# A message-passing layer with gathered and copied rows: two more tiles copied, and a load moved ahead of two stores

## The chip, the cores and the metric

The kernel runs on one core of one Trainium2 chip. The metric is the device time of one execution in microseconds (us), the median of several runs. A core has five engines that run their own instruction streams and meet at semaphores: TensorE (PE in the profile, its weight loads PEld), VectorE (DVE), ScalarE (ACT), GpSimd (POOL) and SyncE (SP). Here SP issues nearly all plain transfers; GpSimd issues the indirect gathers.

## The reference

There are 12500 nodes with 64 features and 200000 edges, sorted by destination, with 32 features each. Each edge makes a message out of its source's row, its destination's row and its own features; messages are summed at the destinations, each node is updated, and the result is normalized:

```python
msg_in = concat([nodes[row], nodes[col], edge_features])
messages = relu(msg_in @ mW1 + mb1) @ mW2 + mb2
aggregated = segment_sum(messages, col)
upd = relu(concat([nodes, aggregated]) @ uW1 + ub1) @ uW2 + ub2
out = layernorm(x + upd)
```

## The kernel before

**Tiles and groups.** The edges are cut into 1563 tiles of 128, and these into 261 groups of 6 (the last, group 260, has 3). The destinations are sorted, so all edges of a tile fall into a window of 32 nodes. Two tables are made at the start: A = x W1a (for sources) and B = x W1b + b1 (for destinations). For a group, TensorE multiplies one-hot columns of the destinations and the edge features with B's windows and the edge weights (`edge_part`, L367). GpSimd gathers A's rows of the group's 768 sources, one indirect DMA per tile (`gather`, L209), into `xg`. VectorE adds both (L394), ScalarE takes the relu (L395). TensorE then sums the relus into windows of a wide PSUM tile, by a selection matrix (`collect`, counts L424, sums L427).

**Copied tiles.** In some groups, listed in `COPIED`, the last two tiles are not gathered. Their sources' columns of x (a transposed copy lies in SBUF) are copied one by one into a tile `xc`: columns 0 to 63 by ScalarE (`singly`, L338), 64 to 127 by VectorE (`joined`, L345), each after a load of its address into a register (L315). TensorE multiplies `xc` with W1a into the same PSUM tile (L370). In such a group VectorE's add is shorter (L390), and ScalarE has two relus (L391, L392). `COPIED` starts at group 16 and goes on in steps of 3 and 2; before the change it ends at 246, 249, 251, 254. A group's columns are copied over some 2.5 stages, a few stages ahead of it (`portion`).

**Updates.** The nodes are finished in 34 updates (u = 0 to 33). In the end these follow one another every 3 or 4 groups: the sums of update 30 close behind group 250, of 31 behind 254, of 32 behind 257, of 33 behind 260. An update consists of: opening a new PSUM tile (L402, L422) and carrying the overlap of 32 nodes over (`carry`); ScalarE's copies of counts and sums (`close`, L441 and L442); the load of x's columns into `xw` (`columns`, L457, with the first node's number loaded into a register, L455); two dense products (`update`, L464 with `xw` and L465 with the sums); a relu (L470); two products back to rows (`residual`, L478 and L480); `evacuate` (L486), `statistics` (L494, L496), `deviation` (L501), `norm` (L507, L510) and `store` (L518). There are two `xw` tiles, used in turn: update 33 has the one of update 31.

**Order.** The order is written out by hand: a loop over stages s = 0 to 263 issues, on each engine's queue, the relu of group s, the sums of group s - 1, the product of group s + 1, the copies for later groups, and the steps of updates that are due. Gathers run up to some ten groups ahead, as far as buffers are free. SP's queue takes, stage by stage, B's windows (L274), one-hot sources (L225), edge features (L256), columns and stores, in that order of issue. `columns(u)` stands in stage 260 for u = 33, behind the store of update 32; the product of group 254 needs a PSUM slot that the relu (L470) of update 30 frees.

Of the kernel before, what the change touches and what calls it, by code (L numbers as in the profile page):

```python
# [29 lines left out]
NSUB = -(-NT // SUB)  # L30
# [41 lines left out]
YBASE = XBASE + 4 * XCOLS  # L72
FIRST, GAPS = 16, (3, 2)
COPIED = []
while FIRST + sum(GAPS) * (len(COPIED) // len(GAPS)) + sum(GAPS[:len(COPIED) % len(GAPS)]) < NSUB - 6:
    COPIED.append(FIRST + sum(GAPS) * (len(COPIED) // len(GAPS)) + sum(GAPS[:len(COPIED) % len(GAPS)]))
RNDS = -(-len(COPIED) // len(GAPS))
LAST = 4 * (N - 1)
# [3 lines left out]
def updates():  # L82


    def node(s):
        return N * min(1.0, s * SUB * P / E) ** 2
    at = [0]
    for s in range(1, NSUB):
        if s > at[-1] and node(s + 1) - node(at[-1]) > UN - WIN:
            at.append(s)  # L90
    at = [a for a in at if a < NSUB - 32]
    steps = -(-(NSUB - 3 - at[-1]) // 4)
    return at + [at[-1] + -(-(NSUB - 3 - at[-1]) * (i + 1) // steps) for i in range(steps)]


UPD = updates()
# [5 lines left out]
def gnn_kernel(ctx: ExitStack, tc: tile.TileContext, x1T, x, eT, e_rows, src, src_row, dst, dst_row, wlist, wrow, wnext, whalf,  # L102
# [33 lines left out]
    K = len(UPD)  # L136
# [50 lines left out]
    def frees(s):  # L187

        a = (XG + 1) // 2 + s - XG - ROWB
        return min(2 * a + 1, XG - 1) if a < (XG + 1) // 2 else XG + a - (XG + 1) // 2  # L190
# [23 lines left out]
    with tc.tile_pool(name="sup", bufs=2) as sup, tc.tile_pool(name="work", bufs=2) as work, tc.manual_schedule():  # L214
# [33 lines left out]
        def counts(g):  # L248

            SB[g] = S[g].bitcast(BF).rearrange("p k (w h) -> p k w h", h=2)  # L250
# [37 lines left out]
        def columns_list():  # L288

            for r in range(len(GAPS)):  # L290
                v = src_row[:, ((FIRST + sum(GAPS[:r])) * SUB + SUB - 2) * P:]
                nc.sync.dma_start(cols[r * RNDS:(r + 1) * RNDS],
                                  bass.AP(v.tensor, v.offset, [[sum(GAPS) * SUB * P, RNDS], [1, 2 * P]]))
            cv = cols.rearrange("k (b e) -> k b e", b=2)
            for b, base in enumerate((XBASE, YBASE)):
                nc.vector.tensor_scalar(col_a[:, :, b], cv[:, b], 4.0, float(base), op0=ALU.mult, op1=ALU.add)
# [141 lines left out]
        def close(u):  # L438

            ps, pn = sums.pop(u)  # L440
            nc.scalar.copy(xw[u % 2][0:1, :UW], pn)  # L441
            nc.scalar.copy(sums_s[u % 2], ps)  # L442
# [3 lines left out]
        def width(u):  # L446

            return UN if u + 1 < K else UL
# [4 lines left out]
        def columns(u):  # L453

            n0 = nc.values_load(usup[0:1, u:u + 1], engines=[ET.SP], min_val=0, max_val=N - 1,  # L455
                                skip_runtime_bounds_check_because="destinations are node numbers")
            nc.sync.dma_start(xw[u % 2][ONE:, :width(u)], x1T[:, bass.ds(n0, width(u))])  # L457
            us[u] = n0
# [64 lines left out]
        def relative(a, b):  # L523

            wbc = work.tile([P, WCH], I32, name="wbc", tag="tb")
            nc.sync.dma_start(dst_s[:, a:b], dst[:, a:b])
            nc.sync.dma_start(wbc[:, :b - a], wrow[:, a:b].broadcast_to([P, b - a]))
            nc.vector.tensor_tensor(drc[:, a:b], dst_s[:, a:b], wbc[:, :b - a], op=ALU.subtract)

        def halves(a, b):  # L530

            for h in range(2):
                nc.sync.dma_start(wh[64 * h:64 * h + 64, a:b], whalf[h:h + 1, a:b].broadcast_to([64, b - a]))
# [21 lines left out]
        def others(a, b):  # L555

            nc.sync.dma_start(xfull[:D, a:b, HB:], xchunks[:, a:b, HB:])
            nc.sync.dma_start(yfull[D:, a:b, :HB], xchunks[:, a:b, :HB])
            if b == NB // NCH:
                nc.sync.dma_start(xbot[D:, full:], x1T[1:, full:XCOLS])  # L560

        def zeros(i, n):

            w = XCOLS // n
            for t in (xtop[D:], xbot[:D]):
                nc.scalar.activation(t[:, i * w:(i + 1) * w], ident[:D, 0:1].broadcast_to([D, w]), AF.Copy, scale=0.0)
# [100 lines left out]
        def rest(s):  # L667

            if 3 <= s < 9 and s % 2:
                others((s - 3) // 2 * 4, (s - 3) // 2 * 4 + 4)  # L670
            if 3 <= s < 11:
                zeros(s - 3, 8)
            if s == 9:
                columns_list()
            if s == 1:
                relative(8 * SUP, 8 * SUP + WCH)
            elif s == 2:
                relative(8 * SUP + WCH, NT)
                halves(4 * SUP, NTP // 2)
            elif s == BS:  # L680
                nc.sync.dma_start(wa, wrow.rearrange("o (p c) -> (o p) c", c=NSUP))
                nc.sync.dma_start(wb, wnext.rearrange("o (p c) -> (o p) c", c=NSUP))
                nc.scalar.dma_start(w2, mW2)
                nc.scalar.dma_start(u1a, uW1[D:2 * D, :])
                nc.scalar.dma_start(b2c, mb2.rearrange("(f o) -> f o", o=1))
                nc.vector.memset(uz[:D], 0.0)
                nc.vector.memset(ux[:D], 0.0)
                nc.vector.memset(eps, EPS)
                nc.vector.memset(ones, 1.0)
                nc.vector.tensor_copy(ux[D:], ident[D:, D:])  # L690
                nc.scalar.dma_start(uz[D:], uW1[0:D, :])
                nc.scalar.dma_start(ux[ONE:ONE + 1], ub2.rearrange("(o f) -> o f", o=1))
                nc.scalar.dma_start(ub1_s, ub1.rearrange("(f o) -> f o", o=1))
                nc.scalar.dma_start(u2, uW2)
            elif s == BS + 2:
                weights()
                checks()
# [47 lines left out]
        due = {(UPD[u + 1] if u + 1 < K else NSUB) + 1: u for u in range(K)}  # L745
# [10 lines left out]
        for s in range(last + 2):  # L756
            g, j = divmod(s, SUP // SUB)
            while gathered < NSUB and frees(gathered) < s:
                gather(gathered)
                gathered += 1  # L760
            tail = due.get(s - 1) == K - 1

            def earlier(n):

                return next((u for d, u in due.items() if u + 2 < K and s - d == n and (n < 2 or u + 3 < K)), None)
            if tail:
                norm(K - 1)
            if s + 2 < NSUB:
                windows(s + 2)
            if s < NSUB:  # L770
                node_part(s)
                joined(s, 0, 3 if j == 0 and g + 1 < NSUP else 2)
            if s in at_end:
                for stage, u in at_end[s]:
                    stage(u)
            for stage, n in ((evacuate, 2), (statistics, 3), (deviation, 4), (norm, 5)):
                if earlier(n) is not None:
                    stage(earlier(n))
            if 1 <= s <= NSUB:
                collect(s - 1)  # L780
            if s + 1 in due:
                close(due[s + 1])
            if j == 0 and g + 1 < NSUP:
                select(g + 1, s)
                load(g + 1)
                counts(g + 1)
            if j == 1 and g + 2 < NSUP:
                loadd(g + 2)
            if chunks and s >= BS and chunks[0] < NCH + NB * (s + 1 - BS) / (SUP // SUB * (GE - 1) - BS):
                chunk_b(chunks.pop(0), [Bv])  # L790
            if s in due and due[s] + 1 < K:
                carry(due[s] + 1)
            if s in due and due[s] + 2 != K:
                update(due[s])
            if s + 1 < NSUB:
                if s + 1 < XG:
                    transpose(s + 1)
                edge_part(s + 1)
            if earlier(1) is not None:
                residual(earlier(1))  # L800
            if s == UPD[K - 1]:
                update(K - 2)
            if s == UPD[K - 1] + 1:
                residual(K - 2)
            if due.get(s) == K - 1:
                activated(K - 1)
                residual(K - 1)
                statistics(K - 1)
                deviation(K - 1)
            if s + 2 in due:  # L810
                columns(due[s + 2])
            rest(s)
            joined(s, 2 if j == 0 and g + 1 < NSUP else 1, 3 if j == 0 and g + 1 < NSUP else 2)
            singly(s, 0, 1)
            if s in due and due[s] + 2 < K:
                activated(due[s])
            if s == UPD[K - 1]:
                activated(K - 2)
            if tail:
                store(K - 1)  # L820
            if earlier(5) is not None:
                store(earlier(5))
# [170 lines left out]
```

## Time and profile before

| What | us |
|---|---|
| median of 3 runs | 1737.42 |
| lowest and highest run | 1736.82, 1737.85 |
| the profiled execution | 1741.59 |
| its span, first to last instruction | 1739.8 |
| busy TensorE, ScalarE, GpSimd, VectorE | 1448.5, 1468.6, 1301.0, 1056.2 |

The granted clock of TensorE was 0.581 in the mean of the span. How to read the rows below: a row of a timeline has its start and its length in us from the span's start, the engine, the line of the kernel, the operation, what it writes and reads, and in brackets the idle time of the engine before it with what ended it. SPq and POOLq are instructions of a sequencer, which waits or issues. A row of windows has the busy time of each engine in a stretch, and the TensorE clock that was granted in it, where 1.00 is full and 0.50 half. A matmul in 32-bit floats counts as two, so "x12" are a group's 6 tiles.

### The profile page before, as it was taken

What the parts mean: (1) busy time and instruction counts of PE and PEld (TensorE: products, weight loads), DVE (VectorE), ACT (ScalarE), POOL (GpSimd) and SP (SyncE); (2) the same over time, 40 slices, a digit from 0 to 9 for tenths busy, and PEclk for the clock granted to TensorE, in tenths of its full rate; (3) what the DMA queues carried; (4) which work ended last, traced back from release to release, by engine and by line L of the source; (5) the groups of instructions that cost most, each with busy time, mean ns of one, the idle gap of its engine ahead of it and who ended that gap; (6) DMA issues with size and microseconds to landing.
All of it is one profiled execution on the core that took longest, in us unless ns stands there. A gap on an engine that the chain in (4) does not pass through costs nothing.

```text
span 1739.8 us, 46406 instructions
## 1 busy us (share of the span) xinstructions
PE 1448.5 (83%) x9620; PEld 1247.5 (72%) x9620; DVE 1056.2 (61%) x7329; ACT 1468.6 (84%) x6712; POOL 1301.0 (75%) x1380
## 2 busy tenths in 40 slices
PE   3697888888988888887987898888899878899997
PEld 3586777877777767666776776677777767677776
DVE  1526666666665656666665666666667666666643
ACT  0277989999998898998898999998999999899942
POOL 7777777777777777777777777777777777777774
PEclk8585555555555555656555555655556566666656
DMA  8783444433333333333343433443344444443442
GB/s 213 204 175 99 127 112 115 115 97 100 98 101 92 96 97 93 98 102 94 98 107 102 105 108 103 105 107 103 106 106 110 107 109 106 108 112 104 113 112 66
DMA packets 207588, 192.45 MB, mean 111 GB/s; under 512 B 57511, under 2 KB 173409, under 8 KB 207313
## 3 DMA queue, kind: packets, MB, share of 16 engines
q0 software_dynamic: 43872, 87.97, 20.6%
q1 hardware_dynamic: 148896, 92.56, 19.6%
q10 hardware_dynamic: 14546, 8.93, 1.8%
q8 instruction: 91, 1.49, 0.4%
q14 instruction: 183, 1.50, 0.3%
HBM read 171.54 MB, written 17.76 MB: 109 GB/s over the span
## 4 chain that ended last, share of the span: by engine, by line
POOL 41%; issue 24%; DMA 14%; DVE 10%; PE 5%; ACT 2%; DVEq 2%; SPq 1%; ACTq 0%; POOLq 0%
POOL xg L209 41%; DMA xg<-tab_a,src_s 10%; DVE xc L345 3%; DVE h L394 2%; ACT xc L338 2%; PE sums L427 2%; DVEq L315 2%; PE pc L367 1%; DVE l L237 1%; DMA tab_a<-tb 1%; DMA l<-in_dst_row 1%; DMA w1b<-in_mW 1%; DVE h L390 0%; DMA l<-in_eT 0%; DMA xtop<-in_x1T 0%
## 5 line engine op out<-in xcount | busy, mean ns | idle before, releaser
L209 POOL DMA_INDIRECT xg<-tab_a,src_s x1311 | 1242.0, 947 | 399.8 <-issue 372.0
L338 ACT ACTIVATE xc<-xtop,xbot 128x1 f32 x6144 | 1166.2, 280 | 42.2 <-issue 31.7
L345 DVE TENSOR_TENSOR xc<-xtop,xbot 128x1 int32 x6144 | 536.6, 154 | 417.9 <-issue 402.4
L427 PE MATMUL sums<-sel,h 128*128 128x32 f32 x3126 | 638.9, 371 | 20.4 <-ACT h L395 13.9
L427 PEld LDWEIGHTS sums<-sel,h 128*128 128x128 f32 x3126 | 605.3, 294 | 39.1 <-ACT h L395 15.4
L367 PE MATMUL pc<-rhs,l 64*128 64x128 f32 x3126 | 420.0, 415 | 188.7 <-DVE h L394 134.7
L367 PEld LDWEIGHTS pc<-rhs,l 64*128 64x128 f32 x3126 | 349.6, 295 | 253.0 <-DVE h L394 152.3
L395 ACT ACTIVATE h<-h 128x768 f32<-128x768 f32 x156 | 129.6, 831 | 111.6 <-DVE h L394 110.8
L394 DVE TENSOR_TENSOR h<-pc,xg 128x768 f32<-128x768 f32 x156 | 148.0, 949 | 121.8 <-DMA xg<-tab_a,src_s 67.6
L237 DVE TENSOR_TENSOR l<-l,cps 128x768 f32<-128x768 int32 (+1 forms) x134 | 127.8, 953 | 23.4 <-DMA l<-in_dst_row 18.8
L424 PEld LDWEIGHTS <-one 128*1 128x1 bf16 x1563 | 55.9, 83 | 58.7 <-issue 50.7
L424 PE MATMUL cnt<-sel,one 128*1 128x32 bf16 x1563 | 89.2, 187 | 0.4 <-issue 0.3
L390 DVE TENSOR_TENSOR h<-pc,xg 128x512 f32<-128x512 f32 x96 | 66.1, 688 | 25.8 <-DMA xg<-tab_a,src_s 11.5
L243 DVE TENSOR_TENSOR sel<-cps,drc 128x384 f32<-128x384 f32 x131 | 71.6, 547 | 14.9 <-PE sums L427 14.7
L464 PE MATMUL pu<-xw,uz 128*128 128x448 f32 (+1 forms) x68 | 61.8, 1012 | 17.3 <-DVE h L394 13.6
L370 PE MATMUL pc<-w1a,xc 64*128 64x128 f32 x384 | 75.0, 398 | 0.0
L209 POOL DMA_INDIRECT xg<-in_x,src_s x60 | 58.0, 967 | 19.1 <-issue 17.7
L391 ACT ACTIVATE h<-h 128x512 f32<-128x512 f32 x96 | 59.2, 617 | 10.4 <-DVE h L390 9.5
L370 PEld LDWEIGHTS pc<-w1a,xc 64*128 64x128 f32 x384 | 66.7, 311 | 0.0
L583 ACT COPY tb<-pb 128x512 f32<-128x512 f32 (+1 forms) x13 | 7.4, 570 | 58.5 <-DMA tab_a<-tb 26.1
L465 PE MATMUL pu<-sums_s,w2u 128*128 128x448 f32 (+1 forms) x68 | 55.2, 914 | 0.0
L573 PE MATMUL pb<-w1a,xtop 64*128 64x128 f32 x100 | 24.0, 425 | 29.9 <-DVE tb L581 17.9
(104 smaller groups left out, 803.3 us busy)
## 6 DMA issues: line engine op xcount, KB each, us to landing
l<-in_dst_row SPq DMA_DIRECT2D x262, 96.0 KB
l<-in_eT SPq DMA_DIRECT2D x262, 96.0 KB
xg<-tab_a,src_s POOLq DMA_INDIRECT x1311
rhs<-tab_b SPq DMA_DIRECT2D x361, 32.0 KB
tab_b<-tb SPq DMA_DIRECT2D x13, 512.0 KB
rhs<-tab_b SPq DMA_DIRECT2D x387, 16.0 KB
tab_a<-tb ACTq DMA_DIRECT2D x12, 512.0 KB
out<-y SPq DMA_DIRECT2D x33, 128.0 KB
```

What stands on the lines that cost most here:

```text
L209: nc.gpsimd.indirect_dma_start(out=a[:, i, :] if s < XG else a[:, i // 2, i % 2, :], out_offset=None, in_=A[:, :] if s >= XG else x[:, :], ...
L237: nc.vector.tensor_tensor(l[r], l[r].bitcast(I32), node[r].unsqueeze(2).broadcast_to([r.stop - r.start, SUP // 2, P]), op=ALU.is_equal)
L243: nc.vector.tensor_tensor(s[:, :nt], slot.unsqueeze(1).broadcast_to([P, nt, WIN]), drc[:, g * SUP:g * SUP + nt].unsqueeze(2).broadcast_to( ...
L338: nc.scalar.activation(o[:, e:e + 1], top.bitcast(F32), AF.Identity, bias=bot.bitcast(F32))
L345: nc.vector.tensor_tensor(o[:, e:e + 1].bitcast(I32), top.bitcast(I32), bot.bitcast(I32), op=ALU.bitwise_or)
L367: nc.tensor.matmul(pc[:, b, k, :], L[g][q:q + 64, m, :], rhs[g % 2][q:q + 64, w, :], start=s >= XG or k == 0, stop=s >= XG and not copied)
L370: nc.tensor.matmul(pc[:, b, k, :], xc[s][q:q + 64], w1a[q:q + 64], start=False, stop=True)
L390: nc.vector.tensor_tensor(h[:, :, :m], pc[:, :, :m], a[:, :, :m], op=ALU.add)
L394: nc.vector.tensor_tensor(h[:, b, :m], pc[:, b, :m], a[:, b, :m], op=ALU.add)
L395: nc.scalar.activation(h[:, b, :m], h[:, b, :m], AF.Relu)
L424: nc.tensor.matmul(pn[:, bass.ds(ws[i], WIN)], one, SB[g][:, k0 + i, :, 1], start=False, stop=ends and i == n - 1)
L427: nc.tensor.matmul(ps[:, bass.ds(ws[i], WIN)], h[:, i % 2, i // 2, :], S[g][:, k0 + i, :], start=False, stop=ends and i == n - 1)
```

## The change

The bound of the list of copied groups goes from `NSUB - 6` to `NSUB - 4` (NSUB is 261), so that one more group is listed: 256. Its first four tiles are gathered, its last two copied by columns, in stages 251 to 253. The load of the addresses has 49 rows instead of 48 for each of its two halves. And `columns` of the last update is issued in stage 258 (`UPD[K - 1]` is 258) in place of stage 260; of the other updates it stays where it was.

```diff
-... < NSUB - 6:
+... < NSUB - 4:
     COPIED.append(FIRST + sum(GAPS) * (len(COPIED) // len(GAPS)) + sum(GAPS[:len(COPIED) % len(GAPS)]))
...
-            if s + 2 in due:
+            if s + 2 in due and due[s + 2] + 1 < K:
                 columns(due[s + 2])
+            if s == UPD[K - 1]:
+                columns(K - 1)
             rest(s)
```

More of the change, by code (lines that the diff above doesn't have):

```diff
@@ L74 @@
 COPIED = []
-while FIRST + sum(GAPS) * (len(COPIED) // len(GAPS)) + sum(GAPS[:len(COPIED) % len(GAPS)]) < NSUB - 6:
+while FIRST + sum(GAPS) * (len(COPIED) // len(GAPS)) + sum(GAPS[:len(COPIED) % len(GAPS)]) < NSUB - 4:
     COPIED.append(FIRST + sum(GAPS) * (len(COPIED) // len(GAPS)) + sum(GAPS[:len(COPIED) % len(GAPS)]))
```

## The prediction

> **What bounds the kernel now.** I read the page first: its groups, then its chain.
>
> ```profile
> span 1739.8 us, 46406 instructions
> ...
> L209 POOL DMA_INDIRECT xg<-tab_a,src_s x1311 | 1242.0, 947 | 399.8 <-issue 372.0
> ```
>
> GpSimd issues 1311 gathers of the table (60 more read x). Each takes 947 ns and is followed by an idle 0.30 us that waits for nothing, as POOL's timeline at the end shows, so the gathers follow one another every 1.25 us. 1371 of them make 1714 us of the 1739.8: the body is paced by the number of gathers.
>
> ```profile
> 1717.14 0.95 POOL L209 DMA_INDIRECT xg<-tab_a,src_s  x1 [0.30 <-DMA xg<-tab_a,src_s]
> 1718.39 0.94 POOL L209 DMA_INDIRECT xg<-tab_a,src_s  x1 [0.30 <-issue]
> 1719.64 0.94 POOL L209 DMA_INDIRECT xg<-tab_a,src_s  x1 [0.30 <-issue]
> ```
>
> What follows the last gather comes from the chain in order of time (start, length, what):
>
> ```profile
> 1719.64 2.88 DMA xg<-tab_a,src_s
> ...
> 1725.54 0.99 DVE y L510 x4
> ...
> 1726.65 0.41 SPq L518
> ...
> 1727.57 1.88 DMA xw<-in_x1T
> 1729.44 0.14 issue
> 1729.58 1.19 PE pu L464 x2
> ```
>
> The gather lands at 1722.5; the update before the last (u = 32) is normalized and stored; behind that store, on SP's queue, goes the load of x's columns for the last update (u = 33); its landing releases TensorE. The chain leaves out what else TensorE had to do, so its timeline comes next (start, length, idle before):
>
> ```profile
> 1666.26 0.58 PE L402 MATMUL sums<-zero_b 128*128 128x480 bf16 x1
> ...
> 1670.84 1.86 PE L464 MATMUL pu<-xw,uz 128*128 128x448 f32 x2
> ...
> 1674.12 1.65 PE L367 MATMUL pc<-rhs,l 64*128 64x128 f32 x12
> ...
> 1678.66 1.81 PE L367 MATMUL pc<-rhs,l 64*128 64x128 f32 x12
> 1680.11 0.80 PE L370 MATMUL pc<-w1a,xc 64*128 64x128 f32 x4
> 1680.83 1.97 PE L478 MATMUL py<-ux,xw 128*128 128x64 f32 x8
> ...
> 1684.43 0.32 PE L424 MATMUL cnt<-sel,one 128*1 128x32 bf16 x6
> ...
> 1687.39 1.65 PE L367 MATMUL pc<-rhs,l 64*128 64x128 f32 x12
> 1688.97 0.33 PE L424 MATMUL cnt<-sel,one 128*1 128x32 bf16 x6
> ...
> 1715.55 1.86 PE L464 MATMUL pu<-xw,uz 128*128 128x448 f32 x2
> ...
> 1720.65 0.71 PE L367 MATMUL pc<-rhs,l 64*128 64x128 f32 x6
> ...
> 1723.22 0.30 PE L424 MATMUL cnt<-sel,one 128*1 128x32 bf16 x6
> ...
> 1725.06 0.85 PE L427 MATMUL sums<-sel,h 128*128 128x32 f32 x6
> 1729.58 1.19 PE L464 MATMUL pu<-xw,uz 128*128 128x256 f32 x2 [3.66 <-DMA xw<-in_x1T]
> ```
>
> No idle time stands in it between 1666 and 1725.9; then 3.66 us for the columns. The windows say at which clock (busy times of PE, PEld, DVE, ACT, POOL; PEclk is third from the end):
>
> ```profile
> 1628.00:1636.00 8.00, 7.88 (x81) 7.06 (x80) 5.20 (x37) 8.00 (x41) 5.87 (x8) 0.95 0.42 110
> 1648.00:1656.00 8.00, 8.00 (x81) 7.12 (x80) 4.68 (x44) 7.83 (x39) 5.87 (x8) 0.92 0.44 114
> 1666.00:1676.00 10.00, 10.00 (x49) 6.38 (x48) 4.24 (x24) 5.02 (x18) 7.56 (x9) 0.50 0.44 113
> ...
> 1706.00:1717.00 11.00, 11.00 (x60) 9.69 (x61) 3.08 (x12) 2.11 (x4) 8.40 (x9) 0.50 0.41 103
> 1718.00:1726.00 8.00, 7.92 (x74) 6.83 (x72) 4.26 (x20) 3.32 (x9) 1.98 (x3) 1.00 0.17 41
> ```
>
> So two bounds run nearly together to the end: the gathers, and a TensorE that is fully busy, at half clock up to 1717. This decides what the second edit is worth.
>
> **The columns ahead of the stores.** The load moves from stage 260 to stage 258, so on SP's queue it comes behind the loads of operand 130 and ahead of the stores of updates 31 and 32. Its instructions are one register load and one DMA; nothing is added. SP is idle there:
>
> ```profile
> 1715.35 0.79 SPq L256 DMA_DIRECT2D l<-in_eT  x2
> 1722.06 5.00 SPq L518 DMA_DIRECT2D out<-y  x2
> 1727.57 0.40 SPq L457 DMA_DIRECT2D xw<-in_x1T  x1
> ```
>
> It would be issued at about 1716.5 and, with the 1.88 us seen above, land at about 1718.5. Its buffer was last read by the residual of update 31, earlier in TensorE's order than group 257's sums, so it should not wait; were it to wait, the store of update 31 would be queued behind it, but that store waits for its y until 1722 anyhow. The wait of 3.66 us goes. What is late next are ScalarE's two copies of the closed sums, and TensorE's own queue:
>
> ```profile
> 1725.19 0.53 ACT L441 COPY xw<-cnt 1x480 f32<-1x480 f32 x1
> 1725.95 0.56 ACT L442 COPY sums_s<-sums 128x480 f32<-128x480 f32 x1 [0.23 <-PE sums L427]
> ```
>
> The first matmul pair (L464) needs the counts, done at 1725.72, and a free TensorE, 1725.91. The second (L465) starts 0.98 later, when the sums, done at 1726.51, are there. So this edit alone is worth 3.7 us here. If it changed nothing it would be worth 0; I see no row for a loss.
>
> **Group 256 with two copied tiles.** Removed: two gathers, 2 x 1.25 = 2.5 us; those of groups 257 to 260 all come 2.5 us earlier. Added on TensorE: four L370 matmuls. Group 254's product, which has them, takes 1680.83 - 1678.66 = 2.17 us, group 255's, which has not, 1688.97 - 1687.39 = 1.58: 0.59 us at half clock. Added on ScalarE and VectorE: 64 columns each, spread over stages 251 to 253 (14, 26, 24).
>
> ```profile
> 1659.77 4.93 ACT L338 ACTIVATE xc<-xtop,xbot 128x1 f32 x26
> ...
> 1674.23 0.63 ACT L470 ACTIVATE hTu<-pu,ub_s 128x448 f32<-128x448 f32 x1 [3.65 <-PE pu L465]
> ...
> 1682.52 0.37 ACT L392 ACTIVATE h<-pc 128x256 f32<-128x256 f32 x1
> ```
>
> At 4.93 / 26 = 0.19 us a column ScalarE gets 12.1 us more between 1669 and 1685, where it now waits. Its relus come later by parts of that, but TensorE lags: group 254's relu ends at 1682.9, and its sums begin at 1688.97, 6 us later. The tightest place is L470 of update 30: the 14 and 26 columns ahead of it are 7.6 us, the 3.65 us it waits now cover a part, so it ends at about 1674.86 + 7.6 - 3.65 = 1678.8, and the product of group 254 takes the PSUM slot that it frees, at 1678.66 now. That is 0.2 us or so of stall; if the cover were gone (TensorE ahead by then) up to 2 us, but then TensorE has that time to spare. VectorE's 64 columns lie in waits for gathers in the same way; taken at nothing.
>
> How much of the 2.5 us reaches the end depends on TensorE.
> - It never catches up: nothing is gained and the four matmuls cost 0.59. Sum -3.66 + 0.59 = -3.1.
> - It has caught up by group 259: that group's h is added 2.5 us before the 1718.61 below, the product of group 260 can then start at 1718.61 - 2.5 + 0.96 = 1717.1, and what follows (half a product, a residual, one and a half group's sums) takes at full clock 1725.91 - 1720.65 = 5.26 us; at half clock 0.79 + 3.60 (1680.83 to 1684.43) + 1.5 x 2.96 (1684.43 to 1687.39) = 8.83. At half clock it ends at 1725.9, as now, and the sum is -3.7. At full clock it ends at 1722.4, the copied counts (1725.72 - 2.5) are the later, L464 starts at 1723.3: -6.3.
>
> ```profile
> 1718.61 0.96 DVE L394 TENSOR_TENSOR h<-pc,xg 128x768 f32<-128x768 f32 x1 [3.11 <-DMA xg<-tab_a,src_s]
> ```
>
> **Sum.** Of the three ends I take the middle one, since most windows of these last 50 us show 0.50, and add a fifth of the step to the third for a stretch of full clock that falls in part into those 8.83 us: -3.7 - 0.5 = -4.2 us. The profiled execution took 1741.59 us (its span and 1.8 around it), 4.2 more than the median of the runs, 1737.42; I take the difference over to the median: 1733.2.
>
> **Rivals.**
> 1. TensorE stays behind to the end (-3.1, 1734.3). For it: 51 us without a gap. If the closing stretch also runs at half clock as it does not in this execution, L464 now starts 6.36 us after the residual's end (1723.22 to 1729.58) and would start 1.5 x 2.96 = 4.44 after it: 1.9 less 0.59 is a gain of 1.3, 1736.1.
> 2. TensorE at full clock through the tail: -6.3, 1731.1. The rows speak both ways: 0.95 and 0.92 in the windows at 1628 and 1648, 0.50 in the next 51 us, two dense updates among them. [...]
> 3. Slower: the full clock that now begins near 1717.4 does not come. It follows the dense products of update 32 at 1715.55, and the four added matmuls push these to 1716.1. At half clock follow 3.28 (1670.84 to 1674.12), 4.58 for opening and summing a group (1666.26 to 1670.84) and 8.83: 1732.8, which is 3.2 us after today's 1729.58, so 1740.6. It decides once the last sums end over 3.7 us later than now. [...]
> 4. The change doesn't do what it says: excluded, as the order of the new kernel's instructions has 1309 gathers and the load ahead of the stores.
>
> **How the numbers follow.** A measurement tells about 0.2%, 3.5 us. The forecast, -3.5 to -5: 0.45. Rival 1: 0.31. Rival 2: 0.17. Rival 3: 0.05; ScalarE's and VectorE's columns holding TensorE up by more than a microsecond, which I cannot price closer than 0 to 2 us: 0.02. Faster by over 0.2%: 0.45 + 0.17 and little else, 0.61. Within 0.2%: rival 1 and the last case, 0.33. Slower: 0.06. The range runs from rival 2 to the half-clock end of rival 1: 1731.0 to 1736.0, and leaves out rival 3.
>
> **What would show it.** The load of xw issued near 1716.5, no wait of L464 for it; the last gather issued at 1717.1; four more L370; L464 at 1725 to 1726 with ScalarE's copies or TensorE's queue before it; and PEclk of 1700 to 1726, which says which case it is. I am wrong if L464 starts after 1727 (clock) or if TensorE shows waits for L470 or the relus between 1672 and 1690.

## The result and the profile after

| | before | after |
|---|---|---|
| median, us | 1737.93 (18 runs) | 1733.37 (18 runs) |
| lowest and highest run | 1736.82, 1738.50 | 1729.50, 1735.44 |
| ratio of the times, 95% interval | | 0.9972 [0.9965, 0.9979] |
| the profiled execution | 1741.59 | 1733.92 |
| its span | 1739.8 | 1732.1 |
| last gather issued, in the span | 1719.64 | 1713.83 |
| L464 of the last update, in the span | 1729.58 | 1722.43 |

The changed kernel is faster by 0.28% (0.21 to 0.35%), 4.6 us between the medians, and its runs are spread over 5.9 us where those of the kernel before lie within 1.7.

The page of the changed kernel, its span and the group of the gathers:

```profile
span 1732.1 us, 46562 instructions
...
L209 POOL DMA_INDIRECT xg<-tab_a,src_s x1309 | 1237.2, 945 | 399.0 <-issue 367.9
```

There are two gathers fewer, and the mean of one is 945 ns where the execution before had 947. Two nanoseconds look like nothing, but there are 1309 of them. The timeline of POOL gives the last one:

```profile
1713.83 0.95 POOL L209 DMA_INDIRECT xg<-tab_a,src_s  x1 [0.30 <-issue]
```

It is issued 5.81 us earlier than before. Two gathers of 1.25 us are 2.5 of it; the other 3.3 are the pace of all of them, 1.2493 us from one to the next in place of 1.2518 (the mean over POOL's timeline, without the few gaps of over 1.4 us near the start). The first two experiments bear on this pace: it differs between executions, and is not the change's doing. From the last gather to L464 of the last update it is now 8.6 us, and was 9.9: 1.3 less. From there to the end of the span it is 9.7 in place of 10.2; the remaining 0.6 us are not the change's either, since the traces of the experiments that leave these steps as they were have 9.2 to 10.0 there, with the columns ahead of the stores or behind them. So the two traces show 2.5 + 1.3 = 3.8 us of the change and 3.9 us that are not its doing; together the 7.7 by which the spans differ.

Where the 1.3 come from is seen in the timeline of SP (start, length, what):

```profile
1709.58 0.79 SPq L256 DMA_DIRECT2D l<-in_eT  x2
1710.93 0.36 SPq L457 DMA_DIRECT2D xw<-in_x1T  x1
1716.49 11.92 SPq L518 DMA_DIRECT2D out<-y  x3
```

The load of the columns goes out ahead of the three stores, 11.5 us before it is needed. In the chain of work that ended last, in order of time, it no longer appears:

```profile
1702.59 2.66 DMA xg<-tab_a,src_s
...
1705.38 0.97 DVE h L394
...
1706.39 1.66 PE pc L367 x12
1708.05 1.84 PE pu L464 x2
...
1718.33 2.70 PE sums L427 x12
...
1722.62 1.01 PE pu L464 x2
```

The chain leaves the gathers at the one that lands at 1705.25, the last of group 258. VectorE adds it, and from 1706.39 to the last update it is TensorE's own queue without a gap, as its timeline shows (the bracket is the idle time before the row). It is a near thing: VectorE's add of group 259 ends at 1714.00, 0.05 us before the product of group 260 (the row at 1714.05).

```profile
1706.39 1.66 PE L367 MATMUL pc<-rhs,l 64*128 64x128 f32 x12 [2.90 <-DVE h L394]
1708.03 1.86 PE L464 MATMUL pu<-xw,uz 128*128 128x448 f32 x2
...
1712.13 1.52 PE L427 MATMUL sums<-sel,h 128*128 128x32 f32 x12
...
1714.05 0.71 PE L367 MATMUL pc<-rhs,l 64*128 64x128 f32 x6
...
1718.26 2.77 PE L427 MATMUL sums<-sel,h 128*128 128x32 f32 x12
...
1722.43 1.20 PE L464 MATMUL pu<-xw,uz 128*128 128x256 f32 x2
```

Look at the two L427 rows: the same twelve matmuls take 1.52 us at 1712 and 2.77 at 1718. The windows say why (PE, PEld, DVE, ACT, POOL busy; PEclk third from the end):

```profile
1691.00:1701.00 10.00, 9.24 (x85) 7.63 (x84) 3.55 (x9) 2.56 (x5) 7.56 (x9) 0.99 0.40 102
1702.00:1711.00 9.00, 6.11 (x24) 4.05 (x24) 3.08 (x12) 1.99 (x4) 6.87 (x8) 0.50 0.37 89
1712.00:1715.00 3.00, 2.98 (x32) 2.64 (x29) 0.96 (x1) 0.96 (x3) 2.17 (x3) 1.00 0.25 68
1716.00:1727.00 11.00, 10.18 (x49) 9.14 (x48) 3.60 (x21) 2.98 (x8) 0.00 (x0) 0.50 0.13 26
```

TensorE has caught up with the gathers (it waits 2.90 us at 1706.39); at 1691 to 1701 it had the full clock, where the execution before shows 0.50 all the way from 1666 to 1717. Its closing run goes at half clock, with one stretch at full clock, from 1711.6 to 1715.0. ScalarE's two copies stand close ahead of the last update, but do not hold L464 up:

```profile
1721.24 0.55 ACT L441 COPY xw<-cnt 1x480 f32<-1x480 f32 x1 [1.51 <-PE cnt L424]
1722.66 0.56 ACT L442 COPY sums_s<-sums 128x480 f32<-128x480 f32 x1 [0.87 <-PE sums L427]
```

### The profile page after: what moved, and what is told of

It is laid out like the page before. It is cut to its first block, busy times and chain, and to the rows that moved or that the text cites. A ratio compares the mean times of both kernels' runs of the same rounds, so it can differ in the third digit from the quotient of the medians.

```text
span 1732.1 us, 46562 instructions
## 1 busy us (share of the span) xinstructions
PE 1458.2 (84%) x9624; PEld 1257.6 (73%) x9624; DVE 1063.1 (61%) x7393; ACT 1480.2 (85%) x6777; POOL 1295.9 (75%) x1378
## 4 chain that ended last, share of the span: by engine, by line
POOL 39%; issue 23%; DVE 13%; DMA 11%; PE 9%; DVEq 3%; ACT 2%; ACTq 0%; SPq 0%; POOLq 0%
POOL xg L209 39%; DMA xg<-tab_a,src_s 10%; DVE xc L345 6%; DVE h L394 3%; PE sums L427 3%; DVEq L315 3%; PE pc L367 2%; DVE l L237 2%; ACT xc L338 2%; PE pu L464 1%; DVE h L390 1%; PE pu L465 1%; DVE y L510 1%; PE py L478 1%; PE py L480 1%
## 5 line engine op out<-in xcount | busy, mean ns | idle before, releaser
L338 ACT ACTIVATE xc<-xtop,xbot 128x1 f32 x6208 | 1178.6, 280 | 45.7 <-issue 33.3
L345 DVE TENSOR_TENSOR xc<-xtop,xbot 128x1 int32 x6208 | 543.3, 154 | 419.8 <-issue 407.1
L427 PE MATMUL sums<-sel,h 128*128 128x32 f32 x3126 | 642.8, 372 | 20.4 <-ACT h L395 13.7
L427 PEld LDWEIGHTS sums<-sel,h 128*128 128x128 f32 x3126 | 609.0, 296 | 40.0 <-ACT h L395 15.4
L395 ACT ACTIVATE h<-h 128x768 f32<-128x768 f32 (+1 forms) x155 | 128.7, 831 | 101.7 <-DVE h L394 98.8
L394 DVE TENSOR_TENSOR h<-pc,xg 128x768 f32<-128x768 f32 (+1 forms) x155 | 147.1, 950 | 106.3 <-DMA xg<-tab_a,src_s 56.9
L243 DVE TENSOR_TENSOR sel<-cps,drc 128x384 f32<-128x384 f32 x131 | 71.7, 547 | 11.5 <-PE sums L427 11.2
L464 PE MATMUL pu<-xw,uz 128*128 128x448 f32 (+1 forms) x68 | 58.4, 959 | 14.5 <-DVE h L394 14.5
L465 PE MATMUL pu<-sums_s,w2u 128*128 128x448 f32 (+1 forms) x68 | 52.5, 873 | 0.0
L478 PE MATMUL py<-ux,xw 128*128 128x64 f32 x268 | 50.1, 347 | 0.8 <-DVE h L394 0.8
```

The source lines that it names most:

```text
L338: nc.scalar.activation(o[:, e:e + 1], top.bitcast(F32), AF.Identity, bias=bot.bitcast(F32))
L345: nc.vector.tensor_tensor(o[:, e:e + 1].bitcast(I32), top.bitcast(I32), bot.bitcast(I32), op=ALU.bitwise_or)
L394: nc.vector.tensor_tensor(h[:, b, :m], pc[:, b, :m], a[:, b, :m], op=ALU.add)
L395: nc.scalar.activation(h[:, b, :m], h[:, b, :m], AF.Relu)
L427: nc.tensor.matmul(ps[:, bass.ds(ws[i], WIN)], h[:, i % 2, i // 2, :], S[g][:, k0 + i, :], start=False, stop=ends and i == n - 1)
L464: nc.tensor.matmul(pu, uz, xw[u % 2][:, :n], start=True, stop=False)
```

## The experiments

A number serves below for all of them: the time from the issue of the last gather to L464 of the last update. It is nearly free of the pace of the gathers. The kernel before had 9.94 us (1729.58 - 1719.64), the changed one 8.60. Each ratio is against the kernel before on the same chip in the same series. There were three series, in which the kernel before had medians of 1740.08, 1738.54 and 1738.02 us; times are compared within a series only. Each experiment's cut of the code is against the changed kernel.

### First series: the two parts, and dense products

**The kernel before once more**, to see what differs between two executions of one kernel.

> The kernel before, once more, for a second trace of it. My theory: the last gather starts near 1716.5 rather than 1719.64, because the first trace had each gather 2 ns longer than the trace of the changed kernel (947 against 945 ns), 3 us over the run, which has nothing to do with the change; the last update's first product (L464) follows the last gather by 9.9 us, as in the first trace (1719.64 to 1729.58), and waits for the load of x's columns. Rival: the 3 us belong to the change, and the last gather starts at 1719.6 again.

One run, 1739.94 us, and only its trace counts here. Its timeline:

```profile
1718.23 0.95 POOL L209 DMA_INDIRECT xg<-tab_a,src_s  x1 [0.30 <-issue]
...
1728.18 1.19 PE L464 MATMUL pu<-xw,uz 128*128 128x256 f32 x2 [3.26 <-DMA xw<-in_x1T]
```

The same kernel issues the same last gather 1.4 us earlier than in the first execution, so the pace is not fixed; but that is less than half of the 3 us that I expected, and this run alone would leave the rest open. The end behind it is 9.95 us again, and L464 waits for the columns again. One thing differs: here TensorE has the full clock from 1702 to 1709 and waits 3.66 us for VectorE's add of group 258 (the product of group 259, at 1711.75). The 51 us without a gap, on which the prediction rests much, belonged to the first execution.

**The columns alone.**

```diff
-... < NSUB - 4:
+... < NSUB - 6:
```

> Only the load of x's columns is moved ahead of the two stores; group 256 is gathered in full. My theory (TensorE's queue is next behind that load): 1.9 us (tail at half clock) to 3.7 us (tail at full clock) faster than before, so 1734.2 to 1736.0, with no wait of L464 for the load, and runs that spread by 2 us or more. Rival A, the stores' order is the whole gain: 4.5 us faster, 1733.4. Rival B, the load was hidden: no change.

1736.87 us (1733.76 to 1739.16), ratio 0.9982 [0.9973, 0.9991]: 3.1 us less (1.6 to 4.7).

```profile
1716.25 0.95 POOL L209 DMA_INDIRECT xg<-tab_a,src_s  x1 [0.30 <-issue]
...
1722.97 1.20 PE L464 MATMUL pu<-xw,uz 128*128 128x256 f32 x2
```

The wait for the columns is gone, and the end behind the last gather is 6.72 us in this execution, 3.2 less than in the kernel before. The gain lies in the 1.9 to 3.7 us that my theory gave; no change at all (rival B) is out, 4.5 us (rival A) lies just inside the interval. The spread is 5.4 us, that of the kernel before in this series 2.8. This run bears on the pace too, and more strongly: with all 1371 gathers, and an edit that begins only at stage 258, it issues the last gather 3.4 us earlier than the first execution of the kernel before.

**The copies alone.**

```diff
-            if s + 2 in due and due[s + 2] + 1 < K:
+            if s + 2 in due:
                 columns(due[s + 2])
-            if s == UPD[K - 1]:
-                columns(K - 1)
```

> Only group 256's two tiles are copied; the columns are loaded behind the stores as before. My theory: the chain of the update before the last, its store and the columns stays in place and is paced by the last gather where TensorE is in time, so 0 to 2.5 us faster, likeliest 1.5, 1736.4. Rival A, gathers pace everything: 2.5 us faster, 1735.4. Rival B, TensorE never catches up and its four added products count: 0.6 us slower.

1737.11 us (1734.52 to 1738.54), ratio 0.9985 [0.9976, 0.9994]: 2.6 us less (1.0 to 4.2), by its middle nearer to the full 2.5 of two gathers than to the 1.5 that I held likeliest; the interval holds both, and the trace decides.

```profile
1713.20 0.95 POOL L209 DMA_INDIRECT xg<-tab_a,src_s  x1 [0.30 <-issue]
...
1723.10 1.19 PE L464 MATMUL pu<-xw,uz 128*128 128x256 f32 x2 [4.32 <-DMA xw<-in_x1T]
```

Here too the end is 9.90 us. In three executions with the columns behind the stores it is 9.94, 9.95 and 9.90: with a wait of 3.3 to 4.3 us for the columns TensorE has that much to spare, and what the gathers give is had in full. (The spread of the times, 4.0 us, lies between that of the kernel before and that of the columns alone; the profiles don't say why.) Alone the parts give 3.1 and 2.6, together 5.7; the changed kernel did not run in this series, and its three ratios (0.9972, and 0.9961 and 0.9968 in the series below) are 4.9, 6.8 and 5.6 us. Within the intervals the parts add.

**Dense products of zeros behind two updates,** to see whether full clock comes ahead of the last groups.

```diff
             nc.tensor.matmul(pu, w2u, sums_s[u % 2][:, :n], start=False, stop=True)
+            if u in (K - 4, K - 3):
+                for _ in range(3):
+                    nc.tensor.matmul(sums[u + 1][0], zero_b[:, :P], zero_b, start=False, stop=False)
```

> The changed kernel with three products of zeros (480 columns in bf16, added to the open sums, which they do not change) behind the dense products of updates 30 and 31, so that a stretch of dense work there lasts over 6 us. [...] The products cost 3 x 0.5 us at half clock each time; a full-clock window saves 2.3 us or more: 1 to 3 us faster than the changed kernel, 1730.5 to 1732.5, with less spread, and 1.00 in PEclk behind both updates. Rival, TensorE's clock does not set the tail: no change or up to 3 us slower, the same spread.

1732.43 us (1731.46 to 1736.01), ratio 0.9959 [0.9946, 0.9973]. The products cost 1.4 us each time:

```profile
1673.11 1.41 PE L468 MATMUL sums<-zero_b 128*128 128x480 bf16 x3
...
1700.49 1.40 PE L468 MATMUL sums<-zero_b 128*128 128x480 bf16 x3
...
1724.64 1.20 PE L464 MATMUL pu<-xw,uz 128*128 128x256 f32 x2
```

Full clock came behind both, from 1674.4 for 3.4 us and from 1701.7 for 6.8, but did not last into the closing run, which had one stretch of its own, of 3.4 us; the end was 9.21 us (1724.64 less the last gather at 1715.43). The 2.3 us that full clock was to save each time had no row behind them; here a group's product, counts and sums take 2.56 us at full clock (1701.82 to 1704.38) and 4.54 at half (1686.14 to 1690.68), 1.98 less. The trace is of the slowest of the five runs, 1736.01 us. The time can't be told from the changed kernel's, and neither can the spread.

### Second series: what sets the end now

**The changed kernel again.**

> The changed kernel once more, as the yardstick for the others on this chip. My theory: 4.5 us faster than before with a spread of 4 us or more, and no gain from a stretch of gathers: where the last gather lies in the trace, the last update's first product (L464) follows it by 6.5 to 9.5 us, by how TensorE's clock falls, and not by the fixed 9.9 us of the traces with the columns behind the stores.

1731.87 us (1729.46 to 1734.25), ratio 0.9961 [0.9947, 0.9974]. Timeline and windows:

```profile
1707.14 1.65 PE L367 MATMUL pc<-rhs,l 64*128 64x128 f32 x12 [4.08 <-DVE h L394]
...
1714.25 0.95 POOL L209 DMA_INDIRECT xg<-tab_a,src_s  x1 [0.30 <-issue]
...
1720.34 1.22 PE L464 MATMUL pu<-xw,uz 128*128 128x256 f32 x2
```

```profile
1712.00:1718.00 6.00, 6.00 (x60) 5.32 (x58) 2.74 (x8) 1.94 (x4) 2.59 (x3) 1.00 0.31 76
1719.00:1726.00 7.00, 5.09 (x19) 4.43 (x18) 3.01 (x18) 2.07 (x5) 0.00 (x0) 0.50 0.10 21
```

The same kernel, with its last gather at 1714.25 in place of 1713.83, has an end of 6.09 us where the first execution had 8.60. The stretch of full clock began at 1711.8 (1711.6 in the first) and lasted 6.8 us in place of 3.4. I expected 6.5 to 9.5; 6.09 is below that. A difference of 2.5 us in the end is of the size of half the spread, 4.8 us.

**Two gathers fewer in group 258,** whose last two tiles get no source rows at all.

```diff
+LEFT = (258,)
...
-        return tiles(s)[:SUB - 2 * (s in COPIED)]
+        return tiles(s)[:SUB - 2 * (s in COPIED or s in LEFT)]
...
-                if s in COPIED:
+                if s in COPIED or s in LEFT:
```

> The changed kernel without the gathers of group 258's last two tiles and with nothing in their place (these tiles' messages lack the source's part, and ScalarE's relu is in two parts as in a copied group). My theory, TensorE's queue sets the tail once group 258's product is free to go: the gathers of 258 to 260 land 2.5 us earlier, but TensorE gets no less work, so 0 to 2 us faster than the changed kernel, likeliest 1. Rival, gathers pace the tail to the end: 2.5 us faster than the changed kernel.

1731.47 us (1727.63 to 1731.92), ratio 0.9954 [0.994, 0.9967], 0.4 us less than the changed kernel beside it. The intervals of the two ratios are too wide to exclude the rival's 2.5 us; what follows rests on the trace.

```profile
1711.48 0.94 POOL L210 DMA_INDIRECT xg<-tab_a,src_s  x1 [0.30 <-issue]
...
1711.70 0.71 PE L368 MATMUL pc<-rhs,l 64*128 64x128 f32 x6 [1.45 <-DVE h L395]
...
1715.93 2.77 PE L428 MATMUL sums<-sel,h 128*128 128x32 f32 x12
...
1720.11 1.20 PE L465 MATMUL pu<-xw,uz 128*128 128x256 f32 x2
```

The gathers end 2.8 us earlier than in the run beside it, and the last update (here L465) starts 0.2 us earlier: behind the last product (L368) the sums went at half clock, 2.77 us a group. In this execution the gathers alone no longer set the end.

**No sums of group 259,** which takes a group's sums out of TensorE's closing run.

```diff
+            if s == 259:
+                return
```

> The changed kernel without TensorE's sums and counts of group 259 (its messages are left out of the result); all gathers stay. My theory, TensorE's queue sets the tail: its 1.7 us at full clock to 3.0 us at half clock come off, about 2.3 us faster than the changed kernel, and L464 then follows the last gather by some 6.5 us. Rival, gathers pace the tail to the end: no change, since group 260's gathers, which are the last, still have to land and be added.

1731.1 us (1730.45 to 1732.55), ratio 0.9958 [0.9945, 0.9972]: 0.8 us less than the changed kernel beside it, where I expected 2.3. What took the rest:

```profile
1714.12 1.17 PE L367 MATMUL pc<-rhs,l 64*128 64x128 f32 x6 [1.69 <-DVE h L394]
...
1721.04 1.22 PE L466 MATMUL pu<-xw,uz 128*128 128x256 f32 x2 [0.56 <-ACT xw L443]
```

The trace is of the slowest of the five runs. With less to do TensorE waits 1.69 us for VectorE's add of group 259, so for a gather, then 0.56 for a copy of ScalarE, and what stands between goes at half clock. TensorE, the gathers and the copies lie within 2 us of one another here: taking away from one of them alone gives a part only.

**Products of zeros all through the end**: three more in each of the last four updates, two ahead of the sums of each of the last three groups, two behind the residual of update 32.

```diff
             nc.tensor.matmul(pu, uz, xw[u % 2][:, :n], start=True, stop=False)
+            for _ in range(3 if u >= K - 4 else 0):
+                nc.tensor.matmul(pu, zero_b[:, :P], zero_b[:, :n], start=False, stop=False)
...
+            for _ in range(2 if s >= NSUB - 3 else 0):
+                nc.tensor.matmul(ps, zero_b[:, :P], zero_b, start=False, stop=False)
...
                 residual(K - 2)
+                for _ in range(2):
+                    nc.tensor.matmul(sums[K - 1][0], zero_b[:, :P], zero_b, start=False, stop=False)
```

> The changed kernel with more zero products (bf16, added to open sums or to the dense products themselves, which they do not change): three inside each of the dense products of updates 30 to 33, two in the sums of groups 258 to 260, two behind the residual of update 32. They add about 2 us of work at full clock to the last 12 us, and keep the share of streaming columns up. [...]

1731.42 us (1731.19 to 1732.34), ratio 0.996 [0.9946, 0.9973].

```profile
1707.00:1713.00 6.00, 6.00 (x20) 2.86 (x20) 2.18 (x12) 1.88 (x5) 4.59 (x5) 0.50 0.39 104
1713.00:1726.00 13.00, 11.44 (x96) 9.43 (x95) 5.60 (x27) 4.70 (x11) 1.08 (x2) 0.99 0.15 32
```

In this trace the clock is 0.99 from 1713 to 1726, where the changed kernel beside it has 1.00 from 1712 to 1718 and 0.50 from 1719 to 1726; the spread is 1.15 us, that of the changed kernel beside it 4.8. The small spread agrees with the spread being the clock's; that is not shown, since one run of five was traced and five runs each tell little of a spread. I expected 2 to 4 us less than the changed kernel beside it, but the median is the same: the end behind the last gather is 8.44 us, since the added products themselves take some 2.9 us of the closing run up to L464 (1.1 of them at half clock, in update 32). They buy no time, and perhaps steadiness.

### Third series: the queue's order

**The changed kernel a third time.**

> The changed kernel as the yardstick on the chip of this job: 0.3 to 0.4% faster than before, L464 of the last update 6 to 9.5 us behind the last gather.

1732.34 us (1730.46 to 1734.59), ratio 0.9968 [0.9958, 0.9978]; the end behind the last gather is 7.97 us (1721.98 - 1714.01). TensorE waits 0.91 us at group 259's product here.

**One more copied group,** 259.

```diff
-... < NSUB - 4:
+... < NSUB - 1:
```

> The changed kernel with group 259 copied as well: its last two tiles' gathers go, so that groups 259 and 260 come 2.5 us earlier, while group 258, behind whose add TensorE's closing run of 15 us begins in the traces, comes no earlier; TensorE gets four more products. My theory, that run sets the tail: between 0.6 us slower and 1 us faster than the changed kernel. Rival, the last gather paces the tail: 2.5 us faster.

1738.35 us (1735.21 to 1741.24), ratio 1.0004 [0.9995, 1.0013]: 6 us more than the changed kernel beside it, which neither theory had.

```profile
1705.52 0.96 DVE L394 TENSOR_TENSOR h<-pc,xg 128x768 f32<-128x768 f32 x1 [4.01 <-DMA xg<-tab_a,src_s]
...
1706.53 1.97 PE L478 MATMUL py<-ux,xw 128*128 128x64 f32 x8 [4.65 <-DVE h L394]
...
1710.39 2.77 PE L427 MATMUL sums<-sel,h 128*128 128x32 f32 x12
1713.09 1.81 PE L367 MATMUL pc<-rhs,l 64*128 64x128 f32 x12
...
1729.49 1.20 PE L464 MATMUL pu<-xw,uz 128*128 128x256 f32 x2
```

In the changed kernel the residual of update 31 (L478) starts at 1698.87, and the product of group 259 waits for VectorE's add of group 258. Here the residual waits for that add, 4.65 us, and the product behind it does not. Residual and product take their PSUM tiles from the same two slots; the reading is that the residual now has the slot that group 258's product filled. So the residual and a group's sums, done while TensorE waited anyhow, fall behind the wait: 6.56 us of them (1706.53 to 1713.09), and from there to L464 it is 23.0 us (1706.53 to 1729.49) in place of 16.0 (1706.39 to 1722.43). Why the slots come out another way was not settled.

**The update before the last done earlier,** with the sums ahead of it, while TensorE waits for group 258; the residual of update 31 has a slot of the sums, as that of update 32 had already.

```diff
-            py = psum.tile([P, UB, D], F32, name="py", tag="sums" if u + 2 == K else "pc")
+            py = psum.tile([P, UB, D], F32, name="py", tag="sums" if K - 3 <= u < K - 1 else "pc")
...
+            if s == UPD[K - 1]:
+                collect(s - 1)
+                close(K - 2)
+                update(K - 2)
             if s < NSUB:
                 node_part(s)
...
-            if s == UPD[K - 1]:
-                update(K - 2)
```

> The changed kernel with update 32's close and dense products issued ahead of group 258's add and relu, so that they fill the 3 to 4 us for which TensorE waits for that add in three of the traces (group 259's product, 2.90, 4.08 and 2.98 us); the residual of update 31 takes a slot of the other PSUM pair so that no slot ties them to it. My theory, TensorE's run after that wait sets the tail: up to 3.3 us comes off it where it is long, nothing where L464 already follows the last gather by 6.1 us; 1 to 2 us faster in the median, and L464 at most 8 us behind the last gather. Rival, the tail is paced by the last gather, or by the clock alone: no change.

1732.64 us (1731.53 to 1734.23), ratio 0.9971 [0.9959, 0.9983], no gain over the changed kernel beside it, where I expected 1 to 2 us. The end behind the last gather is 7.71 us, inside the 8 that I gave. One window of the traced run shows the clock:

```profile
1705.00:1724.00 19.00, 18.46 (x94) 15.61 (x93) 7.85 (x33) 5.41 (x12) 7.54 (x8) 0.50 0.25 61
```

3.3 us of work left the closing run, which in the first trace of the changed kernel had a stretch of full clock (1.00 from 1712 to 1715). Here the clock is 1.00 from 1691 to 1704 and 0.50 from 1705 to 1724, so the whole closing run goes at half. In the changed kernel the stretch stood behind the dense products of update 32, which left the closing run too; whether it went with them no run shows.

**Both of these together.**

```diff
-... < NSUB - 4:
+... < NSUB - 1:
```

on top of the edit above.

> Both: update 32 earlier and group 259 copied. My theory: with TensorE's closing run shortened the last gathers' landing counts again, so the two together are worth more than their sum: 2 to 4 us faster than the changed kernel. Rival: no better than update 32 earlier alone, or worse by the four products.

1733.34 us (1729.42 to 1734.89), ratio 0.9967 [0.9955, 0.9979].

```profile
1701.49 1.10 PE L478 MATMUL py<-ux,xw 128*128 128x64 f32 x8
...
1706.88 1.83 PE L464 MATMUL pu<-xw,uz 128*128 128x448 f32 x2 [1.70 <-issue]
...
1711.88 0.94 POOL L209 DMA_INDIRECT xg<-tab_a,src_s  x1 [0.30 <-issue]
...
1723.36 1.20 PE L464 MATMUL pu<-xw,uz 128*128 128x256 f32 x2
```

With its PSUM tile among the sums, the residual of update 31 waits for nothing, and the time is 5.0 us below that of group 259 alone. That agrees with the reading on the slots, but the edit also moves update 32, so it is no proof. The gathers end 2.1 us earlier than in the changed kernel beside it and it gains nothing: the end behind them is 11.48 us, TensorE's queue. The dense products of update 32 (L464, at 1706.88) do not fill the wait here, as they were meant to: they start 0.1 us behind VectorE's add of group 258, which ends at 1706.78. The profile names no releaser for their 1.70 us. No kernel of these is clearly better than the changed one.

## Why the prediction was right

**The columns.** Right: issued behind the loads of operand 130 and ahead of the stores, no wait of L464 for them, TensorE's queue and ScalarE's copies next. The start I gave for it, 1716.5, was that of the execution before; it was 1710.93, since the gathers and all that follows them came earlier. The other signs stand shifted in the same way: the last gather at 1713.83 in place of 1717.1, L464 at 1722.43 in place of 1725 to 1726.

**The three ends.** The prediction put L464 at 1725.9 (half clock) or 1723.3 (full clock) behind a last gather at 1717.1: 8.8 or 6.2 us. The three executions of the changed kernel have 8.60, 7.97 and 6.09. So both ends are real, with the same kernel between them, and the middle one that I took holds for the profiled execution. A stretch of full clock in the closing run, for which the forecast adds a fifth of the step, is in all three; it lasted 3.4 us in the first trace and 6.8 in the second. The fifth itself had no row behind it, and that the sum came so near is in part luck: the runs, 1729.5 to 1735.4, reach from below the full-clock rival's 1731.1 nearly to the slowest case of the first rival, 1736.1.

**TensorE catches up.** Right: it waits 2.90, 4.08 and 0.91 us at group 259's product, where rival 1 had it stay behind to the end. But what let it catch up is not in the working: a stretch of full clock between 1691 and 1709 (0.99 from 1691 to 1701 in the first trace of the changed kernel, 0.99 from 1691 to 1704 in the second), which the first execution of the kernel before lacked (0.50 from 1666 to 1717) and its second had (1702 to 1709). The prediction took its half-clock case because most windows showed 0.50; at 0.50 alone TensorE had not caught up in the first execution.

**The copies.** The size of their share was argued from TensorE alone. By themselves they give the 2.5 us of the two gathers, because the late columns leave TensorE room. Behind the other edit the sum had about 0.5 us for them. The times don't settle that: the changed kernel's 4.9 us less the 3.1 of the columns alone are 1.8, with an uncertainty as large. In the traces, L464 comes 0.5, 2.6 and 1.0 us earlier than in the one of the columns alone (1722.43, 1720.34 and 1721.98 against 1722.97). The four added matmuls are there (388 in place of 384).

**L470 and the PSUM slot.** Wrong. I let the product of group 254 wait for the slot that L470 frees. Timelines of the changed kernel:

```profile
1673.33 0.96 DVE L394 TENSOR_TENSOR h<-pc,xg 128x768 f32<-128x768 f32 x1 [0.35 <-DMA xg<-tab_a,src_s]
...
1673.99 0.61 ACT L470 ACTIVATE hTu<-pu,ub_s 128x448 f32<-128x448 f32 x1
...
1674.35 1.81 PE L367 MATMUL pc<-rhs,l 64*128 64x128 f32 x12 [1.23 <-DMA rhs<-tab_b]
```

The product starts at 1674.35, before L470 ends at 1674.60, so it does not need what L470 frees. Its row names a load of B's windows; its first weight load waited 1.3 us for VectorE's add of group 253, which ends at 1674.29, and in the second trace of the changed kernel its row names that add (1.66 us). So the slot is likely the one of group 253's product. ScalarE's added columns do delay L470, from the end of L465 at 1670.43 to 1673.99, but TensorE needs its result only at 1678.28 (L480). The columns are hidden, as said, but not by the working given; what the text ahead of the prediction says of that slot is wrong with it.

**The sum.** Forecast -4.2 us; the first traces show -3.8 up to L464 without the pace, the medians -4.6. The 4.2 us by which the profiled execution stood above the median were carried over without a reason. Most of it likely has one now: 3.3 us are that execution's pace against that of the changed kernel's trace, whose 1733.92 us lie near its median. No median run of the kernel before was traced. The carrying over did no harm because the change does not touch the pace.

**Slower (rival 3).** In no run of the changed kernel. A stretch of full clock that does not come, as it has it, is seen in the trace of the update done earlier (0.50 from 1705 to 1724), where 3.3 us less work in the closing run bought nothing.

## What to carry to other kernels

When two traces are compared, first take out what belongs to the execution: here the pace of 1370 gathers, read from the start of the last one, was 3.3 of 7.7 us. Where a late transfer is what ends last, the engine behind it has room, and other savings can count in full, as the copies did here (2.6 us, with a wait of 4.32 for the columns); once it is taken away, the next bounds can lie within a microsecond or two of one another, as here, and each further saving alone gives a part. An edit that only adds an entry to a list can still move a wait to an operation that the diff does not name, as with group 259, where 4.65 us fell to the residual: look at the waits of those operations too.

## What the runs showed of the hardware

**The pace of the gathers** differs between executions. In the first trace of the kernel before it was 1.2518 us from one to the next and the last of 1371 was issued at 1719.64; the second trace of the same kernel issues it at 1718.23, the columns alone, with as many gathers, at 1716.25, so 3.4 us lie between them. In the changed kernel it was 1.2493 us in the first trace, and the last of 1369 was issued at 1713.83, 1714.25 and 1714.01 in the three. What sets it no row shows.

**Full clock came in stretches.** In the first trace of the kernel before the last 70 us have one, of 10.2 us (from 1717.5), in that of the changed kernel three, of 3.4, 10.2 and 3.4 us (from 1670.6, 1691.1 and 1711.6). In another execution of the same kernel they had other lengths: the one in the closing run of the changed kernel lasted 3.4 us in the first trace and 6.8 in the second, and the end behind the last gather was 8.60 and 6.09 us. When such a stretch comes, and how long it lasts, no run here explains.

**The busier stretch had the lower clock.** TensorE busy for 18.46 of 19 us, much of it with narrow sums (32 columns to each load of weights), was at 0.50 (the update done earlier); busy for 11.44 of 13 us, with products of 256 to 480 columns among the sums, it was at 0.99 (products of zeros all through the end). So busy time alone does not tell these two apart; what does is not shown, since more than one thing differs between them.
